# Second attention of a fused transformer block: row sums by halving additions on GpSimd instead of matmuls with ones

## The chip, the cores and the metric

The kernel runs on one core of one Trainium2 chip. The core has five engines with a queue each: TensorE (PE; its weight loads are shown as PEld), VectorE (DVE), ScalarE (ACT), GpSimd (POOL) and SyncE (SP), which only issues transfers here. Each engine takes its instructions in a fixed order and waits on semaphores for the others. The metric is device microseconds (us) of one execution; the time of a kernel is the median of its runs.

## The reference

Two layers are applied to x of 16 sequences x 128 tokens x 256 channels. The first is an attention with two key/value sources and a gated feed-forward. The second is a plain masked attention of 32 heads of 8 channels, with 8 groups of keys and values (4 heads share one), and a mixture of experts. The change lies in the second attention alone:

```
def _L1_xattn_ref(Q, K, V, attention_mask, w_q, w_k, w_v, w_o, b_o):
    ...
    scores = jnp.einsum('bnghd,bmgd->bnghm', q, k) / scale
    pad = (attention_mask == 0)[:, None, None, None, :]
    scores = jnp.where(pad, NEG_INF, scores)
    causal = jnp.tril(jnp.ones((S, S), bool))[None, :, None, None, :]
    scores = jnp.where(causal, scores, NEG_INF)
    attn = jax.nn.softmax(scores, axis=-1)
    out = jnp.einsum('bnghm,bmgd->bnghd', attn, v).reshape(B, S, D)
    return out @ w_o.T + b_o
```

The softmax needs, for each of 16 x 128 x 32 rows of 128 scores, the sum of the exponentials; the output of a head is divided by it.

## The kernel before

The kernel works through four parts: the first attention (to about 950 us), the first feed-forward (to about 1080 us), the second attention (to about 1390 us) and the experts. In the second attention a loop runs over 64 steps, n = 0 to 63, and each step handles 8 heads (two groups of 4) of one sequence: sequence b = n // 4, channel half c = n // 2 % 2. In step n the loop emits, in this order: scores(n), top(n), probs(n - 1), exp(n), values(n - 2), and between them keys for a later sequence, the projections of the next group of four sequences, the output of an earlier one, and pieces of the routing. A scheduler then places the instructions of each engine by its own estimate of their times, so the order on an engine can differ a little from the order of the program; after that the order is fixed.

What each function does, with the lines of the profile:

- keys (L973 to L987): GpSimd writes kb, the keys masked for each of the 4 heads of a group (two multiplications L975 for each sequence, two buffers); TensorE projects the values, VectorE copies them into vpad (L986), where each head has its 8 columns of 32 and the rest is zero.
- scores (L989): TensorE adds the mask with an identity matmul (L997) and multiplies queries and kb (L1004) into a PSUM tile of 128 x 1024, two buffers.
- top (L1011): VectorE takes the negated maximum of each of the 8 rows of 128.
- exp (L1020): ScalarE, eight activations of 128 x 128, writes e (three buffers). The queries are on the partitions.
- probs (L1031, L1032): TensorE transposes the eight blocks of e, VectorE copies them to eT.
- values (L1035 to L1054), only for odd n, for the 16 heads of steps n - 1 and n: the loop over t, h and q (L1043 to L1051) multiplies eT with vpad for t = 0 and with ones8 for t = 1, in four column tiles of 32. So the second half of the PSUM tile o holds the sum of exponentials of each head, repeated over its 8 rows, with the channels on the partitions. VectorE takes its reciprocal (L1053) and multiplies (L1054) into oT.
- output (L1060 and after): TensorE multiplies oT with the output weights once per sequence; VectorE adds bias and residual (L1062, L1066).
- load (L906 to L916): the mask of four sequences is loaded as integers into mi, VectorE turns it into pad (0 or -1e30, L915) and combines it with the causal mask (L916).

Besides, GpSimd normalises rows for the next group (L934) and issues the scatter of routed rows (L845).

Of the kernel before, what the change touches and what calls it, by code (L numbers as in the profile page):

```python
# [9 lines left out]
F32 = mybir.dt.float32  # L10
# [3 lines left out]
I32 = mybir.dt.int32  # L14
AF = mybir.ActivationFunctionType
ALU = mybir.AluOpType
AX = mybir.AxisListType

P = 128
# [5 lines left out]
NEG = -1e30  # L25
# [10 lines left out]
def flamingo_kernel(  # L36
# [27 lines left out]
    nc = tc.nc  # L64
# [4 lines left out]
    NH, NG, HD = 32, 8, 8  # L69

    const = ctx.enter_context(tc.tile_pool(name="const", bufs=1))
    small = ctx.enter_context(tc.tile_pool(name="small", bufs=3))
    psum0 = ExitStack()
    psum = psum0.enter_context(tc.tile_pool(name="psum", bufs=2, space=bass.MemoryType.PSUM))
# [14 lines left out]
    def ps_pv(shape):  # L89
        return ps("pv", shape, 1)  # L90
# [11 lines left out]
    def kpn(ap):  # L102
        return ap.rearrange("(k p) n -> p k n", p=P)
# [7 lines left out]
    ident = const.tile([P, P], F32, name="ident")  # L111
# [127 lines left out]
    with (  # L239
# [74 lines left out]
        class Unit:  # L314
# [15 lines left out]
            def load(self):  # L330
                b = self.b
                if self.cross:
                    cx = ap.tile([P, KD, P], F32, tag="ctx", name="ctx")
                    nc.sync.dma_start(out=cx, in_=kpn(ctxT)[:, :, b * P : (b + 1) * P])
                    xx = ap.tile([P, KD * P], F32R, tag="xx", name="xx")
                    nc.sync.dma_start(out=xx.bitcast(F32), in_=xqx[b])
                    self.kv_lhs = [cx[:, k, :] for k in range(KD)]
                    self.q_lhs = [xx[:, k * P : (k + 1) * P] for k in range(KD)]
# [148 lines left out]
            def top(self, c):  # L487
                mx = small.tile([P, 4], F32, tag="mx", name="mx")
                nc.vector.tensor_reduce(mx, self.sc[c], AX.X, ALU.max, negate=True)  # L489
                self.mx = mx  # L490

            def exp(self, c):
                pscore = self.sc.pop(c)
                sums = small.tile([P, 4], F32, tag="sums", name="sums")
                e = ap.tile([P, 4, P], F32, tag="e", name="e", bufs=3)
                for j in range(4):
                    nc.scalar.activation(  # L497
                        e[:, j, :], pscore[:, j, :], AF.Exp, bias=self.mx[:, j : j + 1],
                        accum_out=sums[:, j : j + 1],
                    )  # L500
                self.e[c] = (e, sums)
# [5 lines left out]
            def divide(self, c):  # L507
                e, sums = self.e[c]
                nc.gpsimd.tensor_tensor(  # L509
                    e, e, sums[:, :, None].to_broadcast([P, 4, P]), ALU.mult  # L510
                )
# [10 lines left out]
            def values(self, c):  # L522
                eT = self.eT.pop(c)
                pv = ps_pv([P, 4, P])
                for g in range(2):
                    gg = 2 * c + g
                    nc.tensor.matmul(  # L527
                        pv[:, 2 * g : 2 * g + 2, :], self.vt[:, gg * P : (gg + 1) * P],
                        eT[:, 2 * g : 2 * g + 2, :], start=True, stop=True,
                    )  # L530
                self.pv[c] = pv
# [136 lines left out]
    NT = G * P  # L668
# [75 lines left out]
    NQ = NH // NG  # L744
# [9 lines left out]
    for j in range(B):  # L754
# [9 lines left out]
        out=before, in_=ones, pattern=[[1, P]], compare_op=ALU.is_gt, fill=0.0,  # L764
# [20 lines left out]
    def route(b0, G):  # L785
# [73 lines left out]
    cq = f1.enter_context(tc.tile_pool(name="a1c", bufs=1, side="right", reuse_waits="tile"))  # L859
    gp = f1.enter_context(tc.tile_pool(name="a1f", bufs=2, side="right", reuse_waits="tile"))  # L860
# [17 lines left out]
        out=causal, in_=causal, pattern=[[-1, P]], compare_op=ALU.is_ge, fill=NEG,  # L878
# [5 lines left out]
    for q in range(P // 32):  # L884
# [3 lines left out]
            out=rows, in_=rows, pattern=[[-HD, NQ]], compare_op=ALU.is_ge, fill=0.0,  # L888
# [3 lines left out]
            out=rows, in_=rows, pattern=[[HD, NQ]], compare_op=ALU.is_ge, fill=0.0,  # L892
            base=HD - 1, channel_multiplier=-1,
        )

    ones8 = cq.tile([P, NQ, 32], F32, name="ones8")
    vpads = [cq.tile([P, NG, NQ, 32], F32, name=f"vpad{i}") for i in range(2)]
    nc.gpsimd.memset(ones8, 0.0)
    for i in range(NQ):
        nc.gpsimd.memset(ones8[:, i, HD * i : HD * i + HD], 1.0)  # L900
    for t in vpads:
        nc.gpsimd.memset(t, 0.0)

# [2 lines left out]
    def load(g):  # L906
        cT = gp.tile([P, KD, NT], F32, tag="cT", name="cT")
        nc.gpsimd.dma_start(out=cT, in_=kpn(ctxT)[:, :, g * NT : (g + 1) * NT])
        mi = gp.tile([P, NT], I32, tag="mi", name="mi", bufs=1)
        nc.sync.dma_start(  # L910
            out=mi, in_=mask[g * NT : (g + 1) * NT].partition_broadcast(P)
        )
        comb = gp.tile([P, G, P], BF16, tag="comb", name="comb")
        pad = gp.tile([P, NT], F32, tag="pad", name="pad", bufs=1)
        nc.vector.tensor_scalar(pad, mi, 0.0, NEG, ALU.is_equal, ALU.mult)  # L915
        nc.vector.tensor_tensor(  # L916
            comb, pad.rearrange("p (b t) -> p b t", b=G),
            causal[:, None, :].to_broadcast([P, G, P]), ALU.min,
        )
        front[g] = {"cT": cT, "comb": comb}  # L920
# [42 lines left out]
        else:  # L963
            nc.scalar.copy(f[i][:, c, :], pm)

    kbs, vps, es, eTs, oTs, scs, mxs = {}, {}, {}, {}, {}, {}, {}

    def keys(b):

# [46 lines left out]
    def exp(n):  # L1016
        s, mx = scs.pop(n), mxs.pop(n)
        e = ap.tile([P, 8, P], F32, tag="e", name="e", bufs=3)
        for i in range(8):
            nc.scalar.activation(  # L1020
                e[:, i, :], s[:, i // NQ, i % NQ, :], AF.Exp, bias=mx[:, i : i + 1]
            )
        es[n] = e

    def probs(n):
# [9 lines left out]
    def values(n):  # L1035

        if n % 2 == 0:
            return
        b, c = n // 4, n // 2 % 2
        if c == 0:  # L1040
            oTs[b] = ap.tile([P, KD, P], F32, tag="oT", name="oT")
        o = psum.tile([P, 2, P], F32, tag="pv", name="ps_pv", bufs=1)
        for t in range(2):  # L1043
            for h in range(NQ):
                for q in range(4):
                    lhs = ones8[:, h, :] if t else vps[b][:, 4 * c + q, h, :]
                    nc.tensor.matmul(
                        o[32 * q : 32 * q + 32, t, :], lhs,
                        eTs[n - 1 + q // 2][:, q % 2, h, :],
                        start=(h == 0), stop=(h == NQ - 1),  # L1050
                    )  # L1051
        r = ap.tile([P, P], F32, tag="rsum", name="rsum")
        nc.vector.reciprocal(r, o[:, 1, :])  # L1053
        nc.vector.tensor_tensor(oTs[b][:, c, :], o[:, 0, :], r, ALU.mult)  # L1054

    def output(b):
        oT = oTs.pop(b)
# [26 lines left out]
    for g in range(B // G):  # L1084
# [3 lines left out]
        for b in range(g * G, (g + 1) * G):  # L1088
# [8 lines left out]
    ap = f2.enter_context(tc.tile_pool(name="a1", bufs=2, side="right", reuse_waits="tile"))  # L1097
    psum = f2.enter_context(
        tc.tile_pool(
            name="psum1", bufs=1, space=bass.MemoryType.PSUM, reuse_waits="tile"  # L1100
        )
    )


    N1 = 4 * B
    routes = []
    for n in range(-2, N1 + 5):
        if 0 <= n < N1:
            scores(n)
            top(n)  # L1110
        if 0 <= n - 1 < N1:
            probs(n - 1)
        if 0 <= n < N1:
            exp(n)
        if 0 <= n < G:
            down(B - G + n, hd, psum.tile([P, DM], F32, tag="mm", name="ps_mm"))
            if n == G - 1:
                tp.close()
                ep = ctx.enter_context(tc.tile_pool(name="e1", bufs=2, reuse_waits="tile"))
        if 0 <= n - 2 < N1:  # L1120
            values(n - 2)
        m = n + 2
        if m % 4 == 0 and 0 <= m < N1:
            keys(m // 4)
        g, i = divmod(n + 12, 16)
        if 1 <= g < B // G:
            front_step(g, i)
        for stages in routes:
            next(stages, None)
        m = n - 4  # L1130
        if m % 4 == 3 and 0 <= m < N1:
            output(m // 4)
            for b0, count in ROUTES:
                if m // 4 == b0 + count - 1:
                    routes.append(route(b0, count))
    for stages in routes:
        for _ in stages:
# [4 lines left out]
    psum = ctx.enter_context(  # L1142
        tc.tile_pool(
            name="psum2", bufs=2, space=bass.MemoryType.PSUM, reuse_waits="tile"
        )
    )
# [4 lines left out]
    for e in range(NE):  # L1151
# [6 lines left out]
            out=xe, in_=disp[e * CAP : (e + 1) * CAP, :].rearrange("(c p) d -> p c d", p=P)  # L1158
# [5 lines left out]
        for f in range(NFC):  # L1164
            ph = ps_mm([P, CAP])
            for k in range(KD):
                nc.tensor.matmul(
                    ph, w1t[:, k, f * P : (f + 1) * P], xT[:, k, :],
                    start=(k == 0), stop=(k == KD - 1),
# [3 lines left out]
        for c in range(NCC):  # L1173
            po = ps_sc([P, DM])
            for f in range(NFC):
                nc.tensor.matmul(
                    po, hT[:, f, c * P : (c + 1) * P], w2t[:, f, :],
                    start=(f == 0), stop=(f == NFC - 1),
# [6 lines left out]
                out=out_rows,  # L1185
                out_offset=bass.IndirectOffsetOnAxis(
                    ap=xe[:, c, 2 * DM + 1 : 2 * DM + 2].bitcast(I32), axis=0
                ),
                in_=oe[:, c, :],
# [77 lines left out]
```

## Time and profile before

| what | value |
|---|---|
| median of 3 runs | 1541.4 us (1539.36 to 1542.68) |
| the profiled execution's own time | 1540.11 us |
| its span | 1538.2 us |
| mean granted TensorE clock | 0.968 |
| scores L1004, all 256 records | 1080.2 to 1379.5 us |
| L1020 exponentials (ScalarE), 512 | 139.7 us busy, 384 ns mean |
| L1011 maxima (VectorE), 64 | 78.2 us busy, 1222 ns mean |
| L1047 with ones (TensorE), 1024 records | 272 ns median of one, four at a time |
| L1053 reciprocal (VectorE), 32 | 958 ns median |
| L975 kb (GpSimd), 32 | 33.6 us busy, 1067 ns mean |

A line number names a line of the kernel. Each float32 matmul is two records in the trace, and records of TensorE overlap, so their durations don't add up; the distance from one group's start to the next one's tells more. "Idle before" names the engine that released a waiting instruction.

### The profile page before, as it was taken

The numbers are of one execution on the slowest core, as the hardware profiler recorded it, in microseconds if no ns is written. First come the engines' busy times: TensorE is split into PE (matmuls) and PEld (weight loads), VectorE is DVE, ScalarE is ACT, GpSimd is POOL, SyncE is SP. The second block draws the span as 40 slices with busy tenths as digits, with TensorE's granted clock in tenths as the row PEclk, the third lists the DMA queues.
The fourth block names the chain that finished last, engine by engine and source line by source line (L and its number), as shares of the span: only waits on it lengthen the run. The fifth ranks groups of instructions, "written<-read, shape, count | busy, mean of one in ns | idle before, by whom it ended". The sixth has DMA issues, their size and how long they took to land. (4 is left out here: it accounts for less than half of the span.)

```text
span 1538.2 us, 24640 instructions
## 1 busy us (share of the span) xinstructions
PE 1388.1 (90%) x8612; PEld 1009.7 (66%) x8612; DVE 1052.2 (68%) x2788; ACT 814.6 (53%) x2421; POOL 669.5 (44%) x574
## 2 busy tenths in 40 slices
PE   2778889798897999999999986999999999996998
PEld 1567677677675677777777764555556666664887
DVE  8888878878789777676767765433579797883100
ACT  3656566566556676666666662353355454542121
POOL 4576666666766555556565554120021312111111
PEclk9799999999999999999999998999999999996999
DMA  4300000000013100000000003400210100001662
GB/s 122 112 7 18 28 11 32 15 11 22 11 45 100 44 23 22 11 19 15 18 15 18 8 8 110 141 1 0 83 49 9 50 9 36 9 36 63 194 198 67
DMA packets 51115, 68.67 MB, mean 45 GB/s; under 512 B 5291, under 2 KB 37739, under 8 KB 50992
## 3 DMA queue, kind: packets, MB, share of 16 engines
q1 hardware_dynamic: 36912, 41.31, 9.1%
q10 hardware_dynamic: 11456, 17.63, 3.6%
q0 software_dynamic: 2624, 8.16, 1.5%
q8 instruction: 68, 1.11, 0.3%
q14 instruction: 55, 0.45, 0.1%
HBM read 50.53 MB, written 16.81 MB: 44 GB/s over the span
## 5 line engine op out<-in xcount | busy, mean ns | idle before, releaser
L509 POOL TENSOR_TENSOR e<-e,sums 128x512 f32<-128x512 f32 x128 | 139.7, 1092 | 230.8 <-DVE sums L505 120.8
L497 ACT ACTIVATE e<-ps_sc,mx 128x128 f32<-128x128 f32 x512 | 181.3, 368 | 90.1 <-DVE mx L489 82.7
L454 POOL TENSOR_TENSOR raw<-raw,q_r 128x512 f32<-128x512 f32 x192 | 207.9, 1112 | 34.1 <-DVE q_r L180 33.0
L431 DVE BATCH_NORM_STATS2 q_st<-raw 128x6 f32<-128x128 f32 x768 | 174.1, 279 | 66.9 <-ACT raw L422 66.5
L1020 ACT ACTIVATE e<-ps_sc,mx 128x128 f32<-128x128 f32 x512 | 139.7, 384 | 119.1 <-DVE mx L1011 114.1
L565 PE MATMUL ps_acc<-wp,cat 128*128 128x512 f32 x512 | 160.4, 436 | 17.6 <-POOL cat L227 15.5
L463 PE MATMUL ps_tr<-ident,raw 128*128 128x128 f32 x768 | 121.9, 288 | 46.0 <-POOL raw L454 43.8
L227 POOL TENSOR_TENSOR cat<-e_t,e_e 128x1024 fp32r<-128x1024 bf16 x64 | 136.2, 2128 | 53.7 <-DVE e_t L221 52.1
L481 PE MATMUL ps_sc<-kT,qT 128*128 128x128 f32 x1024 | 140.3, 280 | 15.0 <-ACT qT L472 15.0
L481 PEld LDWEIGHTS ps_sc<-kT,qT 128*128 128x128 f32 x1024 | 131.1, 193 | 33.0 <-ACT qT L472 27.0
L463 PEld LDWEIGHTS ps_tr<-ident,raw 128*128 128x128 f32 x768 | 96.0, 147 | 83.3 <-POOL raw L454 58.2
L519 ACT COPY eT<-ps_tr 128x512 f32<-128x512 f32 x128 | 75.4, 589 | 139.0 <-PE ps_tr L517 138.9
L975 POOL TENSOR_TENSOR kb<-kT,hmask 128x512 f32<-128x512 f32 x32 | 33.6, 1067 | 243.9 <-PE ps_sc L1004 184.6
L565 PEld LDWEIGHTS ps_acc<-wp,cat 128*128 128x128 f32 x512 | 95.9, 194 | 57.4 <-POOL cat L227 22.2
L527 PE MATMUL ps_pv<-eT,vt 128*128 128x256 f32 x512 | 132.1, 379 | 1.0 <-DVE cat_y L538 1.0
L422 ACT COPY raw<-ps_mm 128x512 f32<-128x512 f32 x192 | 113.7, 593 | 27.9 <-PE ps_mm L410 24.8
L527 PEld LDWEIGHTS ps_pv<-eT,vt 128*128 128x128 f32 x512 | 95.9, 189 | 31.2 <-issue 9.0
L538 DVE TENSOR_TENSOR cat_y<-ps_pv,r_sm 128x512 bf16<-128x512 f32 x128 | 87.1, 680 | 39.7 <-PE ps_pv L527 39.5
L472 ACT ACTIVATE qT<-ps_tr,hv 128x512 f32<-128x512 f32 x128 | 100.9, 789 | 21.8 <-PE ps_tr L463 19.8
L497 ACT ACTIVATION_READ_ACCUMULATOR e<-ps_sc,mx 128x1 f32 x512 | 105.3, 206 | 0.0
L489 DVE TENSOR_REDUCE mx<-ps_sc 128x4 f32<-128x512 f32 x128 | 87.2, 681 | 23.6 <-PE ps_sc L481 23.6
L1011 DVE TENSOR_REDUCE mx<-ps_sc 128x8 f32<-128x1024 f32 x64 | 78.2, 1222 | 25.0 <-PE ps_sc L1004 23.4
(228 smaller groups left out, 2807.3 us busy)
## 6 DMA issues: line engine op xcount, KB each, us to landing
w1t<-in_w ACTq DMA_DIRECT2D x8, 1024.0 KB, 5.0
w2t<-in_w ACTq DMA_DIRECT2D x8, 1024.0 KB, 5.6
disp<-empty SPq DMA_DIRECT2D x16, 257.0 KB, 8.5
xe<-disp SPq DMA_DIRECT2D x8, 514.0 KB, 3.6
stage<-in_wprojT SPq DMA_DIRECT2D x16, 256.0 KB, 2.7
xg<-in_x SPq DMA_DIRECT2D x4, 512.0 KB, 3.9
xb<-in_x SPq DMA_DIRECT2D x16, 128.0 KB, 2.1
ctx<-in_ctxT SPq DMA_DIRECT2D x16, 128.0 KB, 2.2
```

The source lines that it names most:

```text
L227: nc.gpsimd.tensor_tensor(dst, t[:, part], e[:, part], ALU.subtract)
L422: nc.scalar.copy(raw.rearrange("p h d -> p (h d)"), pm)
L431: nc.vector.bn_stats(self.st[:, 4 * blk + j, :], self.raws[blk][:, j, :])
L454: nc.gpsimd.tensor_tensor(src, src, self.r[:, 4 * blk : 4 * blk + 4, None].to_broadcast([P, 4, P]), ALU.mult,)
L463: nc.tensor.transpose(pt[:, j, :], src[:, j, :], ident)
L472: nc.scalar.activation(dst, pt, AF.Identity, scale=hv[:, col : col + 1], bias=hv[:, col + 1 : col + 2])
L481: nc.tensor.matmul(pscore[:, j, :], qT[:, j, :], self.kT[:, 2 * c + j // 2, :], start=True, stop=True,)
L497: nc.scalar.activation(e[:, j, :], pscore[:, j, :], AF.Exp, bias=self.mx[:, j : j + 1], accum_out=sums[:, j : j + 1],)
L509: nc.gpsimd.tensor_tensor(e, e, sums[:, :, None].to_broadcast([P, 4, P]), ALU.mult)
L527: nc.tensor.matmul(pv[:, 2 * g : 2 * g + 2, :], self.vt[:, gg * P : (gg + 1) * P], eT[:, 2 * g : 2 * g + 2, :], start=True, stop=True,)
L565: nc.tensor.matmul(self.acc, self.cat[c // 2][:, h % 8, :], wpr[self.cross, c][:, j, :, :], start=(h == 0), stop=(h == 15),)
L1020: nc.scalar.activation(e[:, i, :], s[:, i // NQ, i % NQ, :], AF.Exp, bias=mx[:, i : i + 1])
```

## The change

The sums of exponentials are no longer made by TensorE with ones8. Right after the exponentials of a step, GpSimd adds e to itself by halves, from 128 values per row to 16 (512, 256 and 128 elements per partition). For each pair of steps VectorE reduces the 16 left to one and takes the reciprocals of the 16 sums (16 elements); GpSimd repeats each reciprocal 8 times into rr; a new function divide, called one step later than values, transposes rr on TensorE into the free half of the tile o, copies it to SBUF on ScalarE, and VectorE multiplies as before. The ones8 tile and its memsets go. In load, the mask is loaded straight into pad and converted in place.

```
-    ones8 = cq.tile([P, NQ, 32], F32, name="ones8")
     vpads = [cq.tile([P, NG, NQ, 32], F32, name=f"vpad{i}") for i in range(2)]
-    nc.gpsimd.memset(ones8, 0.0)
-    for i in range(NQ):
-        nc.gpsimd.memset(ones8[:, i, HD * i : HD * i + HD], 1.0)
...
-        mi = gp.tile([P, NT], I32, tag="mi", name="mi", bufs=1)
+        pad = gp.tile([P, NT], F32, tag="pad", name="pad", bufs=1)
         nc.sync.dma_start(
-            out=mi, in_=mask[g * NT : (g + 1) * NT].partition_broadcast(P)
+            out=pad.bitcast(I32), in_=mask[g * NT : (g + 1) * NT].partition_broadcast(P)
         )
         comb = gp.tile([P, G, P], BF16, tag="comb", name="comb")
-        pad = gp.tile([P, NT], F32, tag="pad", name="pad", bufs=1)
-        nc.vector.tensor_scalar(pad, mi, 0.0, NEG, ALU.is_equal, ALU.mult)
+        nc.vector.tensor_scalar(pad, pad.bitcast(I32), 0.0, NEG, ALU.is_equal, ALU.mult)
...
     def exp(n):
...
+        if n % 2 == 0:
+            sums[n // 2] = ap.tile([P, 2, 8, 16], F32, tag="part", name="part")
+        half = ap.tile([P, 8, P // 2], F32, tag="half", name="half", bufs=1)
+        nc.gpsimd.tensor_tensor(half, e[:, :, :64], e[:, :, 64:], ALU.add)
+        nc.gpsimd.tensor_tensor(half[:, :, :32], half[:, :, :32], half[:, :, 32:], ALU.add)
+        nc.gpsimd.tensor_tensor(
+            sums[n // 2][:, n % 2], half[:, :, :16], half[:, :, 16:32], ALU.add
+        )
         es[n] = e
...
     def values(n):
...
         b, c = n // 4, n // 2 % 2
+        r = small.tile([P, 16], F32, tag="sum16", name="sum16")
+        part = sums.pop(n // 2)
+        nc.vector.tensor_reduce(r, part.rearrange("p i h t -> p (i h) t"), AX.X, ALU.add)
+        nc.vector.reciprocal(r, r)
+        rr = ap.tile([P, 16, HD], F32, tag="rr16", name="rr16", bufs=1)
+        nc.gpsimd.tensor_copy(rr, r[:, :, None].to_broadcast([P, 16, HD]))
+        o = psum.tile([P, 2, P], F32, tag="pv", name="ps_pv", bufs=1)
+        for h in range(NQ):
+            for q in range(4):
+                nc.tensor.matmul(
+                    o[32 * q : 32 * q + 32, 0, :], vps[b][:, 4 * c + q, h, :],
+                    eTs[n - 1 + q // 2][:, q % 2, h, :],
+                    start=(h == 0), stop=(h == NQ - 1),
+                )
+        pvs[n] = o, rr
+
+    def divide(n):
+
+        if n % 2 == 0:
+            return
+        b, c = n // 4, n // 2 % 2
+        o, rr = pvs.pop(n)
         if c == 0:
             oTs[b] = ap.tile([P, KD, P], F32, tag="oT", name="oT")
-        o = psum.tile([P, 2, P], F32, tag="pv", name="ps_pv", bufs=1)
-        for t in range(2):
-            for h in range(NQ):
-                for q in range(4):
-                    lhs = ones8[:, h, :] if t else vps[b][:, 4 * c + q, h, :]
-                    nc.tensor.matmul(
-                        o[32 * q : 32 * q + 32, t, :], lhs,
-                        eTs[n - 1 + q // 2][:, q % 2, h, :],
-                        start=(h == 0), stop=(h == NQ - 1),
-                    )
-        r = ap.tile([P, P], F32, tag="rsum", name="rsum")
-        nc.vector.reciprocal(r, o[:, 1, :])
-        nc.vector.tensor_tensor(oTs[b][:, c, :], o[:, 0, :], r, ALU.mult)
+        nc.tensor.transpose(o[:, 1, :], rr.rearrange("p h d -> p (h d)"), ident)
+        rT = ap.tile([P, P], F32, tag="rsum", name="rsum", bufs=1)
+        nc.scalar.copy(rT, o[:, 1, :])
+        nc.vector.tensor_tensor(oTs[b][:, c, :], o[:, 0, :], rT, ALU.mult)
...
         if 0 <= n - 2 < N1:
             values(n - 2)
+        if 0 <= n - 3 < N1:
+            divide(n - 3)
```

More of the change, by code (lines that the diff above doesn't have):

```diff
@@ L964, in qk @@
             nc.scalar.copy(f[i][:, c, :], pm)
-    kbs, vps, es, eTs, oTs, scs, mxs = {}, {}, {}, {}, {}, {}, {}
+    kbs, vps, es, eTs, oTs, scs, mxs, sums, pvs = {}, {}, {}, {}, {}, {}, {}, {}, {}
     def keys(b):
```

## The prediction

> **What bounds the kernel now.** First the page: engine totals and the 40 slices.
>
> ```profile
> PE 1388.1 (90%) x8612; PEld 1009.7 (66%) x8612; DVE 1052.2 (68%) x2788; ACT 814.6 (53%) x2421; POOL 669.5 (44%) x574
> ...
> PE   2778889798897999999999986999999999996998
> POOL 4576666666766555556565554120021312111111
> ```
>
> TensorE is busy for nine tenths of the span. The changed lines run in slices 29 to 36 (38.5 us each), where GpSimd's digits are 0 to 3. The stage window says the same; columns after the stretch are busy us and instructions:
>
> ```profile
> core 0: us, PE busy (x) PEld busy (x) DVE busy (x) ACT busy (x) POOL busy (x), PEclk, DMA share, GB/s
> 1080.00:1390.00 310.00, 305.72 (x3273) 188.98 (x3272) 244.15 (x518) 156.86 (x551) 53.18 (x50) 0.99 0.10 35
> ```
>
> In these 310 us TensorE is busy for 306 and GpSimd for 53. Matmul ends are modelled, so 306 alone does not prove a bound; the timeline decides. Columns: start, length, engine, line. This is one pair of steps (n = 32, 33) without extras:
>
> ```profile
> 1239.91 1.13 PE L1004 MATMUL ps_sc<-kb,qT 32*128 32x512 f32 x4
> ...
> 1240.97 1.09 PE L1031 MATMUL ps_tr<-ident,e 128*128 128x128 f32 x8
> ...
> 1242.43 1.13 PE L1004 MATMUL ps_sc<-kb,qT 32*128 32x512 f32 x4
> 1242.44 2.18 ACT L1020 ACTIVATE e<-ps_sc,mx 128x128 f32<-128x128 f32 x8 [2.76 <-DVE mx L1011]
> ...
> 1243.48 1.52 PE L1031 MATMUL ps_tr<-ident,e 128*128 128x128 f32 x8
> ...
> 1244.93 1.08 PE L1047 MATMUL ps_pv<-eT,vpad 128*32 128x128 f32 x32
> ...
> 1245.83 1.06 PE L1047 MATMUL ps_pv<-eT,ones 128*32 128x128 f32 x32
> 1246.81 0.11 PEld L997 LDWEIGHTS <-identb 128*128 128x128 bf16 x2 [0.20 <-issue]
> ...
> 1247.35 1.13 PE L1004 MATMUL ps_sc<-kb,qT 32*128 32x512 f32 x4
> ```
>
> From scores to scores it takes 1247.35 - 1239.91 = 7.44 us, and TensorE goes from group to group with one real stall: the transposes L1031 at 1243.48 last 1.52 us instead of 1.09, because they eat the exponentials as ScalarE makes them (1242.44 to 1244.62); the next group starts 0.31 us after the last. So the chain of a pair is: scores(even), maximum, exp(even), its transposes, values, scores of the next pair. The row sums (second L1047 line) hold TensorE from 1245.83 to 1246.8 and lie on that chain. The reciprocal L1053 and L1054 are waited for by nobody on TensorE in this pair.
>
> [...] 32 records of 0.27 us each pass in 0.9 to 1.0 us. [...] The trace, two true inputs (columns ns min/median/max):
>
> ```profile
> L227 POOL TENSOR_TENSOR xs<-e_t,e_e x16: 1642/1652/2078, 24.7 to 437.0; 128x768 fp32r<-128x768 bf16 x16
> L227 POOL TENSOR_TENSOR xx<-e_t,e_e x16: 669/675/1115, 26.7 to 438.7; 128x256 fp32r<-128x256 bf16 x16
> ```
>
> From 256 to 768 elements it grows by 977 ns: 1.91 ns per element and 186 ns fixed. [...] Four kb multiplications in a row, each with broadcast inputs, give 1.01 us each:
>
> ```profile
> 1023.06 4.03 POOL L975 TENSOR_TENSOR kb<-kT,hmask 128x512 f32<-128x512 f32 x4 [22.78 <-ACT kT L964]
> ```
>
> [...] No overlap with GpSimd adds is in this trace.
>
> **The change, part by part** (against the profiled execution: 1540.1 us, span 1538.2 plus 1.9; the median 1541.4 is 1.3 above it).
>
> *Removed from TensorE:* the ones half of L1047. Vpad half to ones half is 0.90 us, ones half to next group 0.98; I take 0.95. 32 pairs: 30.4 us, on the path. *Added to TensorE:* one transpose per pair, 1.09 / 8 = 0.13 us, 4.2 us in all. *Added to ScalarE:* a 128x128 copy from PSUM, 0.27 us (L150, 128x128). It stands before exp(even) and waits for the transpose that follows the eight of the odd step: S + 1.06 (to the first transpose) + 1.0 (eight of them) + 0.36 (from the new one's start to its reader, estimated from L149 and L150: 0.69 us for four) + 0.25 (the copy) = S + 2.65, against S + 2.53 now (1239.91 to 1242.44; S is the start of scores(even)). That 0.12 replaces the 0.13 in pairs that wait for the exponentials; it is not added twice. Net gain 30.4 - 4.2 = 26.2 us, if no new wait appears.
>
> *VectorE:* loses the 0.96 us reciprocal, gains a reduction of 256 elements (0.42, from L1011's 1.06 ns per element) and a reciprocal of 16 (0.17). Lighter by 0.37 per pair, not the bound: no gain counted. *Mask into pad without mi, ones8 memsets gone, fourth mask load behind two output rows on SP:* the memsets (0.6 us) stand before a 39 us GpSimd wait, the mask is used some 15 steps later: nothing, and at most one late combination (0.7 us).
>
> *GpSimd:* three adds per step. By the fit: 512 elements 1.16, 256 0.68, 128 0.43, plus two waits on itself of 0.05: 2.37 us per step, 152 us over 64 steps, plus 32 copies of 0.25 (memset 128x128 takes 0.20). From 53 to some 213 us of about 290: it fits on average, but order decides. Bounds for a step: 1.01 x 7/4 + 0.3 = 2.05 below (the kb rate); 3.5 above[...].
>
> **The new wait.** In the built order of the changed kernel, VectorE's reduction over a pair's partial sums is often placed straight before the maximum of the next step. VectorE is in order, so a late GpSimd holds that maximum, then the eight exponentials, then TensorE's transposes. For odd n of the form 4k+1 the reduction stands after a later maximum: no harm. For n = 4k+3 it stands before the maximum of 4k+4. In six of those (n = 15, 19, 31, 35, 47, 51) both kb multiplications of a later batch also stand between the adds of step n-1. Time from S of step n-1:
>
> - exp(n-1) ends 2.65 + 2.18 = 4.83; adds start 4.87.
> - GpSimd: 2.37 (adds) + 2.02 (kb) + 2.37 (adds of n) + 0.25 (the copy in between) = 7.01: done 11.88. exp(n) ended at about 8, so the backlog binds.
> - reduction 11.95 to 12.37, 0.30 for the one or two small operations placed after it, maximum to 13.9, exp(n+1) from 13.92.
> - Without it: S of n+1 is 5.14 (end of the transposes, 4.83 + 0.31) + 0.93 (values) + 0.97 (output L1060) + 0.53 (mask L997) = 7.57; VectorE is through L1062, L1066, L132, L133 at about 9.1; exp(n+1) from 10.3.
>
> Loss 3.6 us each, 21.7 for six, with nothing to set against it: the transposes of n+1 follow their exponentials by 0.3 us and all later TensorE work follows them. The same reckoning at n = 23 (four 1.22 us L934 operations between the adds), n = 9 (backlog of the same four earlier, partly covered by L957 projections) and n = 59 (three scatter issues of 0.97 us in the queue) gives about 2.7 each, 8. At n = 11, 27, 39, 43 projections or router work (2 to 5 us of TensorE) cover the lateness; 0 to 0.7 each, none counted. At the end TensorE waits for the last adds, reduction, copy: 2.4 + 0.4 + 0.2 + 0.3 after exp(63) against 2.2 for transposes and both halves of L1047 now: 1.1. Sum of waits 30.8.
>
> Forecast: 1540.1 - 26.2 + 30.8 = 1544.7 on the profiled execution; with 1.3 for the median, 1546. With 2.05 per step each bad pair loses 3.0, the three others 2.2, the end 1.0: 25.6, net -0.6. With 3.5 per step: 5.9 x 6 + 4.5 x 3 + 3 = 52, net +26.
>
> **Rivals.** (a) *Gain stays, waits mostly hidden; faster.* For it: GpSimd is idle 83% of the stage, and the reduction is placed where its producer was thought done. Against: the order is fixed and 7.0 us of queue do not fit into the 4 us before that maximum. The mechanism is GpSimd's speed in those places: the balance tips at about 2.05 us of adds per step; at 1.5 us half of the waits are left, 1541.4 - 26.2 + 15 = 1530; with none, 1515. Its likeliest time is 1530. (b) *GpSimd is the pace.* Adds at 3.5 us: 4 steps need 14 + 2 + 0.5 = 16.5 us against 14.2 that TensorE needs: slower everywhere, 1567. [...] Against: 213 of 290 us by the fit. (c) *A wash:* the waits eat the gain at 2.05 to 2.2 us per step: 1541. (d) *The change doesn't take the sums off TensorE:* excluded, the 512 matmuls are absent from the built order.
>
> **How the numbers follow.** Forecast (moderately slower, 1545 to 1556) 0.40; faster (a) 0.31; wash (c) 0.16; GpSimd-bound (b) 0.13. About 0.2% (3 us) is what a measurement of this kernel can tell from no change. Faster 0.31, within 0.17, slower 0.52. Range of 8 in 10: 1526 (half of the waits) to 1561; the forecast's own range is 1541 to 1557.
>
> **What would show it.** L1047 with vpad alone, about 1 us per pair. Adds of about 1.16, 0.68 and 0.43 us. The maximum waiting for GpSimd's partial sums or the reduction, 3 us or so in six places, and ScalarE's exp behind it. GpSimd about 213 us busy in the stage. Wrong if the reduction waits under 1 us in those places, or if the stage before 1080 us shifts.

## The result, and the profile after

The changed kernel takes 1576.6 us (median of 6 runs, 1571.9 to 1578.0) against 1541.4 us before: ratio 1.0227, 95% interval 1.0212 to 1.0242. It is slower, as forecast, but by 35 us where 5 were forecast. The profiled execution has a span of 1576.2 us (before 1538.2).

The page of the changed kernel, engine totals and slices:

```profile
PE 1390.5 (88%) x7620; PEld 1002.1 (64%) x7620; DVE 1050.9 (67%) x2821; ACT 819.5 (52%) x2452; POOL 835.7 (53%) x793
...
PE   2878798798988999999999978999898899885998
...
POOL 4566666667677555565656552121766766661111
PEclk9999999999999999999999988999998979885999
```

TensorE has 992 matmul records fewer and is busy for as long as before (1390.5 us, then 1388.1): its records have become longer. In the slices of the second attention (29 to 36) its granted clock reads 9, 9, 8, 9, 7, 9, 8, 8 tenths; in the kernel before it reads 9 in all of them. By the clock's records in the trace, in which only full and half occur, it stood at half for 67.9 us of the stage, and for 6.8 us in the kernel before. The window of the stage (length, then busy us and instructions of each engine, clock):

```profile
1084.00:1414.00 330.00, 293.99 (x2191) 169.34 (x2188) 235.08 (x527) 158.24 (x567) 213.34 (x266) 0.90 0.10 33
```

GpSimd is busy for 213 us, as forecast, and TensorE, busy for 306 of 310 us before, now has gaps. The waits of the stage (who waited for what: us, times, longest):

```profile
ACT e L1015 <- DVE mx L1006: 85.0, 48, 6.0
...
DVE sum L1045 <- POOL part L1023: 40.7, 15, 4.1
...
PE ps_tr L1034 <- ACT e L1015: 12.8, 9, 2.0
PE ps_pv L1067 <- POOL rr L1048: 12.2, 7, 3.5
```

VectorE's reduction L1045 waits 40.7 us for GpSimd's adds, and TensorE waits for the exponentials (L1034) and for the repeated reciprocals rr (L1067). One such place in full, the pairs n = 34 and 36 (start, length, engine, line; in brackets the idle time before and its releaser):

```profile
1274.60 1.04 POOL L970 TENSOR_TENSOR kb<-kT,hmask 128x512 f32<-128x512 f32 x1
1274.63 1.30 DVE L1082 SCALAR_TENSOR_TENSOR row<-t,tg,x 128x256 f32<-128x256 f32 x1
...
1276.32 1.26 POOL L1021 TENSOR_TENSOR half<-e 128x512 f32<-128x512 f32 x1
...
1277.77 0.72 POOL L1022 TENSOR_TENSOR half<-half 128x256 f32<-128x256 f32 x1
...
1277.86 0.33 PE L1067 MATMUL ps_pv<-ident,rr 128*128 128x128 f32 x1 [1.26 <-POOL rr L1048]
...
1278.57 0.45 POOL L1023 TENSOR_TENSOR part<-half 128x128 f32<-128x128 f32 x1
1279.06 0.42 DVE L1045 TENSOR_REDUCE sum<-part 128x16 f32<-128x256 f32 x1 [2.46 <-POOL part L1023]
...
1279.68 1.16 DVE L1006 TENSOR_REDUCE mx<-ps_sc 128x8 f32<-128x1024 f32 x1
...
1280.94 2.18 ACT L1015 ACTIVATE e<-ps_sc,mx 128x128 f32<-128x128 f32 x8 [0.76 <-DVE mx L1006]
...
1281.58 2.06 PE L1034 MATMUL ps_tr<-ident,e 128*128 128x128 f32 x8 [1.90 <-ACT e L1015]
...
1283.57 1.94 PE L1052 MATMUL ps_pv<-eT,vpad 128*32 128x128 f32 x32
...
1285.44 1.03 PE L992 MATMUL ps_sc<-comb,identb 128*128 128x512 bf16 x2
```

The chain is the one the prediction drew: adds, reduction (2.46 us late), maximum of n = 36, its exponentials, TensorE's transposes. Three things in it were not drawn. TensorE waits 1.26 us for rr (L1067), whose copy stands in GpSimd's queue behind the first add of the next step. After the second wait, values L1052 last 1.94 us (before: 1.08) and the mask L992 1.03 (0.59). And VectorE's row operation L1082, 0.45 us without adds, lasts 1.30 us beside GpSimd's kb.

The distance from the scores of n to those of n + 2 ("the pair at n"), taken from the timelines, tells where the time is. Clean pairs (n = 2, 10, 14, 18, 26, 30, 34, 42, 46, 50, 58) are 0.2 to 0.9 us shorter than before, eight of the eleven by 0.77 to 0.90. The pairs at 16, 20, 32, 36, 48, 52, the six of the prediction, are 3.4 to 5.2 us longer, those at 8, 24, 60 3.3 to 4.8. From the first scores to those of n = 62 it takes 325.97 us; before, 296.30.

The rest of the 38.0 us between the two spans is not the stage: the first scores start 4.2 us later, and the end takes 4.1 us more. The start varies over the runs below from 1080.7 to 1085.7 us with the work ahead of it unchanged (and the kernel before from 1539.3 to 1547.0 us over a set of 25 runs), so the experiments are compared by the stage, from the scores of n = 0 to those of n = 62, and by pairs. Both come from the one profiled execution, and a single pair can differ by 1.6 us between two executions without any edit near it (run 6 shows why).

### The profile page after: what moved, and what is told of

The parts are those of the page before. It is cut to its first block, busy times and chain, and to the rows that moved or that the text cites. A ratio compares the mean times of both kernels' runs of the same rounds, so it can differ in the third digit from the quotient of the medians.

```text
span 1576.2 us, 23047 instructions
## 1 busy us (share of the span) xinstructions
PE 1390.5 (88%) x7620; PEld 1002.1 (64%) x7620; DVE 1050.9 (67%) x2821; ACT 819.5 (52%) x2452; POOL 835.7 (53%) x793
## 5 line engine op out<-in xcount | busy, mean ns | idle before, releaser
L1021 POOL TENSOR_TENSOR half<-e 128x512 f32<-128x512 f32 x64 | 81.2, 1269 | 120.5 <-ACT e L1015 116.8
L1034 PEld LDWEIGHTS ps_tr<-ident,e 128*128 128x128 f32 x512 | 62.1, 150 | 61.7 <-ACT e L1015 35.0
```

## The experiments

Times are medians; each ratio is to runs of the kernel before on the same chip.

**1. The reduction moved.**

```
-        nc.vector.tensor_reduce(r, part.rearrange("p i h t -> p (i h) t"), AX.X, ALU.add)
+        red = nc.vector.tensor_reduce(r, part.rearrange("p i h t -> p (i h) t"), AX.X, ALU.add)
+        if n + 2 in tops:
+            after(red, tops[n + 2], "the maximum goes first")
```

> Changed kernel, but VectorE's reduction for odd step n is ordered behind the maximum of step n + 2; nothing else is edited. Theory 1 (a late reduction in front of the next maximum stops the exponentials and then TensorE): the six pairs starting at n = 16, 20, 32, 36, 48, 52 and the one at 24 lose their 4 to 6 us, every pair then gains about 0.76 us against the kernel before, the end still costs about 4 us: 1517 to 1530 us. Rival (GpSimd's adds or the new divide path are too slow everywhere, wherever VectorE's reduction stands): above 1555 us.

1556.2 us, ratio 1.0093 (1.0063 to 1.0123); stage 299.8 us, in the profiled execution, which is the fastest of four (1550.9, 1552.2, 1560.1, 1561.1). The order alone is worth 26 us of the stage; but more than half of what was expected is missing, and the time is just above the 1555 us of the rival. The rival's reason, slow everywhere, does not fit the pairs: ten of the eleven clean ones are 0.77 to 0.96 us shorter than before. The pair at 16 is still 3.9 us longer than before. In its trace TensorE's transpose waits 13.6 us in all for rr, which stands in GpSimd's queue behind the next add.

**2. kb moved behind the adds.**

```
+            if 4 * b - 5 in adds:
+                after(ins, adds[4 * b - 5], "the adds go first")
```

> Changed kernel, but both kb multiplications of sequence b stand on GpSimd behind the adds of step 4b - 5 instead of between them. Theory 1 with the prediction's sum: 2.0 us less GpSimd queue in front of the reduction in the six bad places, so these pairs lose about 2.3 us each instead of 4.2 to 5.9: 1560 to 1567 us. Rival (the wait is made by the speed of the adds themselves, kb does not matter): 1574 to 1579 us. Below 1550 us would say that kb is the whole cause.

1568.9 us, ratio 1.0164 (1.0147 to 1.0181). By the traces, only GpSimd's order differs from the changed kernel. The six pairs lose 1.7 to 3.0 us where they lost 3.4 to 5.2, each 1.0 to 2.2 us less: about what was expected of them. The pairs at 40 and 56 lose 3.3 and 2.3 us more instead, and the time stays 2 us above the expected range.

**3. No adds** (the sums of exponentials are left out; a constant takes their place).

```
-        nc.gpsimd.tensor_tensor(half, e[:, :, :64], e[:, :, 64:], ALU.add)
...
-            sums[n // 2] = ap.tile([P, 2, 8, 16], F32, tag="part", name="part")
+            sums[n // 2] = fixed
```

> Changed kernel without the three GpSimd adds per step; the partial sums are a constant tile, so the softmax sums are left out and the output is not divided by the real ones. Reduction, reciprocal, copy, transpose and division stay. Theory 1: only the TensorE gain is left, 26 us: 1513 to 1520 us. Rival (the divide path, that is rr, one transpose, a ScalarE copy in front of the exponentials, eats the gain by itself): above 1530 us.

1511.5 us, ratio 0.9803 (0.9783 to 0.9823); stage 265.6 us, 30.7 less than before, a little more than the 26 expected. No cost of the divide path is to be seen. So the adds, not the rest of the change, cost 325.97 - 265.56 = 60.4 us of the stage. In these are the places that VectorE's reductions get because of the adds: here, where nothing has to be waited for, the scheduler put the one of n = 35 behind the maximum of 38, not in front of that of 36.

**4. The adds alone, read by nobody**, in the kernel before.

```
+        nc.gpsimd.tensor_tensor(half, e[:, :, :64], e[:, :, 64:], ALU.add)
+        nc.gpsimd.tensor_tensor(half[:, :, :32], half[:, :, :32], half[:, :, 32:], ALU.add)
+        nc.gpsimd.tensor_tensor(
+            sums[n // 2][:, n % 2], half[:, :, :16], half[:, :, 16:32], ALU.add
+        )
         es[n] = e
```

> Kernel before with the three GpSimd adds per step put behind the exponentials, their result read by nobody; the sums still come from the matmuls with ones (and the mask is converted in place, to make room). Theory 1: GpSimd's adds harm nobody unless somebody waits for them, so 1539 to 1546 us; kb comes later but is due late. Rival (the adds slow VectorE, ScalarE or the clock [...], or hold e's buffers): 1555 us or more.

1567.6 us, ratio 1.0152 (1.0135 to 1.0169); stage 320.0 us, 23.7 more than before. The theory failed here: with adds for which nobody waits the stage is 24 us longer, although the other engines keep the order of the kernel before, but for a few operations of VectorE some 90 us ahead of the first scores. The pairs name several ways. At 20, 36 and 52 it is 1.4 to 1.5 us each, and this is VectorE: its tensor_scalar over a row, L138, takes 701 ns in the mean where the kernel before has 408. At n = 20, first in the kernel before, then here:

```profile
1184.79 1.37 DVE L138 TENSOR_SCALAR row<-row,ln_mv,ln_r 128x256 f32<-128x256 f32 x4
...
1193.62 2.52 DVE L138 TENSOR_SCALAR row<-row,ln_mv,ln_r 128x256 f32<-128x256 f32 x4
```

With L135, 0.44 instead of 0.17 us, that is 1.42 us, and the pair is 1.42 us longer; at 36 and 52 the same sum comes out within 0.02 us. At 22, 38 and 54 it is 1.6 us each; there one more stretch of 3.4 us at half clock lies in the pair than in the kernel before (see run 6). At 26, 42 and 58, 2.6 to 3.8 us, VectorE waits 3.9 to 5.3 us with the copy L840 into a row tile whose rows GpSimd still has to scatter; the scatters stand between the adds. In the pair at 16 (4.1 us) VectorE waits 1.7 us for the mask, and a stretch at half clock lies there too. The buffers of e, the last of the rivals, were not held: no exponentials start less than 6.4 us after the end of the add that reads e of three steps before, and one takes 0.38 us, as before.

**5. TensorE's wait filled**, in three of the six places, with the other three as control.

```
+        if n - 1 in (16, 32, 48):
+            for _ in range(7):
+                nc.tensor.matmul(
+                    s[:, 0], identb, f["comb"][:, j, None, :].to_broadcast([P, NQ, P]),
+                    start=True, stop=True,
+                )
```

> Changed kernel with seven more mask matmuls (about 0.27 us each, overwritten by the real ones) in front of scores n = 17, 33 and 49 only, that is inside TensorE's wait of about 2 us in the pairs starting at 16, 32 and 48; every engine's order is otherwise the same. The pairs at 20, 36 and 52 are the control. Theory (TensorE's clock falls in a wait and the 4 us of work after it pays for it): the matmuls after the wait go back to full speed (values 0.95 us instead of 1.88, mask 0.53 instead of 0.97) and these three pairs become 1.0 to 1.8 us shorter than in the changed kernel, the controls stay as they are. Rival (the slow records are something else[...]): the three pairs are as long as before or longer, by up to 0.5 us.

A single run, 1569.6 us. The pairs at 16, 32, 48 go from +5.03, +5.15, +4.26 to +3.81, +3.70, +3.08 us: 1.2 to 1.45 us shorter, though TensorE does 1.7 us more. Of the controls 20 and 52 stay within 0.02 us; 36 changes by 0.44. The pairs at 24, 28 and 38, far from the edit, change by 1.2 to 1.3 us as well, so pairs alone would not prove it. The time from the exponentials of n to the scores of n + 2 does not have that doubt: at 16, 32 and 48 it is 5.47, 5.47 and 5.20 us in the changed kernel, 4.25, 4.03 and 4.03 here, and 4.04 without adds (run 3); at 20 and 52 it is 5.47 and 5.46. TensorE at n = 32, first with the wait filled:

```profile
1257.81 1.13 PE L1005 MATMUL ps_sc<-kb,qT 32*128 32x512 f32 x4
1259.42 1.90 PE L1040 MATMUL ps_tr<-ident,e 128*128 128x128 f32 x8 [0.49 <-ACT e L1021]
1261.25 1.08 PE L1058 MATMUL ps_pv<-eT,vpad 128*32 128x128 f32 x32
1262.26 0.61 PE L998 MATMUL ps_sc<-comb,identb 128*128 128x512 bf16 x2
```

and in the changed kernel:

```profile
1258.49 1.13 PE L999 MATMUL ps_sc<-kb,qT 32*128 32x512 f32 x4
1261.61 2.05 PE L1034 MATMUL ps_tr<-ident,e 128*128 128x128 f32 x8 [1.99 <-ACT e L1015]
1263.60 1.94 PE L1052 MATMUL ps_pv<-eT,vpad 128*32 128x128 f32 x32
1265.46 1.03 PE L992 MATMUL ps_sc<-comb,identb 128*128 128x512 bf16 x2
```

The transposes start 7.76 us after the scores of n = 32 in the first and 7.77 in the second: the exponentials are as late. What is gone is the slowness after the wait. The windows of the changed kernel there (stretch, length, TensorE busy, granted clock):

```profile
1258.00:1260.00 2.00, 1.62 (x7) 1.00 0.00 0
1260.00:1262.00 2.00, 0.39 (x2) 0.62 0.00 0
1262.00:1264.00 2.00, 2.00 (x16) 0.50 0.01 4
1264.00:1266.00 2.00, 2.00 (x34) 0.50 0.00 0
1266.00:1268.00 2.00, 2.00 (x7) 0.67 0.03 8
```

With the wait filled every window from 1250 to 1268 us shows 1.00.

**6. The mask edit alone.**

> Kernel before with only the mask edit: loaded into pad and converted in place, no mi. Theory 1: costs nothing, 1539 to 1545 us, every pair as before. Rival (the load that now waits for the combination holds VectorE near n = 16, which made 4 us of the adds-alone run): the pair at 16 becomes about 4 us longer, 1544 us or more.

A single run, 1544.0 us, inside the spread of the kernel before; stage 297.4 us. The pair at 16 is 1.6 us longer, because VectorE waits there for the mask:

```profile
1165.82 0.43 DVE L914 TENSOR_SCALAR pad<-pad 128x512 f32<-128x512 int32 x1 [1.51 <-DMA pad<-in_mask]
```

So some 1.6 of the 4.1 us of that pair in run 4 come from the mask edit and not from the adds. The pair at 22 is 1.6 us shorter and the one at 54 1.6 longer, where no mask is near: behind the router's small matmuls L798 (16 of 128x8) the clock stood at half for 3.4 us, at n = 22 in the kernel before, at n = 54 in this one. Values in the pair at 22, first in the kernel before, then here:

```profile
1195.29 1.94 PE L1047 MATMUL ps_pv<-eT,vpad 128*32 128x128 f32 x32
...
1198.95 1.08 PE L1046 MATMUL ps_pv<-eT,vpad 128*32 128x128 f32 x32
```

TensorE has the same order in both. So 1.6 us at 22, 38 or 54 in one profile are no proof of an edit's effect.

**7. Late reduction, and rr copied by VectorE.**

```
-        nc.gpsimd.tensor_copy(rr, r[:, :, None].to_broadcast([P, 16, HD]))
+        nc.vector.tensor_copy(rr, r[:, :, None].to_broadcast([P, 16, HD]))
```

> The kernel of the first experiment (reduction behind the maximum of n + 2) with the copy rr on VectorE instead of GpSimd. Theory: 16 us of that run were TensorE's transpose waiting for rr at the end of GpSimd's queue; these waits go, 1535 to 1545 us. Rival (what is left there is contention and late transfers, not rr): 1552 us or more.

1546.1 us, ratio 1.0022 (1.0014 to 1.0029), 1 us above the expected range; stage 294.8 us. TensorE's wait for rr falls to 3.0 us. Still 29 us of the adds' cost are there, although hardly anyone waits for their result any more. The clock stood at half for 29.8 us of the stage (2.0 in run 3). One place, at n = 20:

```profile
1173.95 1.03 POOL L977 TENSOR_TENSOR kb<-kT,hmask 128x512 f32<-128x512 f32 x1
1173.97 1.30 DVE L1093 SCALAR_TENSOR_TENSOR row<-t,tg,x 128x256 f32<-128x256 f32 x1
...
1176.25 0.69 DVE L142 TENSOR_SCALAR ln_v<-ln_mv 128x4 f32<-128x4 f32 x1
...
1176.93 1.21 DVE L1015 TENSOR_REDUCE mx<-ps_sc 128x8 f32<-128x1024 f32 x1
```

and the same row operation in run 3, with GpSimd quiet:

```profile
1168.50 0.45 DVE L1078 SCALAR_TENSOR_TENSOR row<-t,tg,x 128x256 f32<-128x256 f32 x1
```

The row operation is 0.85 us longer and ends 0.29 us after GpSimd's kb; L142 lasts 0.69 instead of 0.17 us. Both stand in front of the maximum. In the window 1084 to 1380 us the mean of the row operation is 881 ns here, 757 in the changed kernel, 497 in run 3; that of the maximum (a reduction) is 1206 to 1222 in all of them.

**8. The same with kb behind the adds.**

> As the run before it, and kb behind the adds of step 4b - 5. Theory: with all three waits on GpSimd's queue gone, what is left over the 1511 us without adds is the stretching of VectorE's small operations (about 10 us) and late scatters: 1525 to 1540 us, faster than the kernel before. Rival (GpSimd's throughput): not under 1543 us.

1546.4 us, ratio 1.0012 (1.0003 to 1.0022): the expectation failed, and the time is where the rival put it; kb's place is worth nothing in sum. Only GpSimd's order differs from run 7. At 20, 36, 48 and 52 the row operation is back at 0.45 us, and these pairs are 0.05 to 1.7 us shorter; the one at 40 is 3.7 us shorter. But the one at 16 is 1.4 us longer and the one at 56 6.0: at 56 VectorE's small L844 and L846 take 1.05 and 1.09 us beside the moved kb (0.16 and 0.23 without adds), and the clock falls behind them. The stretching went elsewhere.

**9. Late reduction, rr on VectorE, and the row operation behind the maximum.**

```
+        if 4 * b + 8 in tops:
+            after(ins, tops[4 * b + 8], "the maximum goes first")
...
-        m = n - 4
+        m = n - 5
```

> The kernel with the late reduction and rr on VectorE, and besides the output of a sequence is issued one step later with its row operation (scalar_tensor_tensor, two SBUF inputs) ordered behind the maximum of step 4b + 8. Theory (what is left there is VectorE operations that stand in front of a maximum and are stretched from 0.45 to 1.3 us by a GpSimd instruction running beside them, plus the clock fall after the wait): the pairs starting at 16, 20, 32, 36, 48, 52 lose 0.7 to 2.5 us less, the stage gets about 8 to 12 us shorter, 1534 to 1540 us. Rival (these pairs are held by something else): 1544 us or more.

1539.5 us (20 runs, 1537.3 to 1542.6), ratio 0.9976 (0.9968 to 0.9983): 0.24% faster than the kernel before, the best version found. The stage is 284.7 us, 10.1 less than in run 7, as expected. The six pairs are now 0.3 to 1.5 us shorter than before; those at 22, 38 and 54, where the moved operations gather, are 2.3 to 4.7 us longer, and from the scores of n = 62 to the end it takes 169.5 us instead of 161.8, which gives most of the stage's gain back. The edit moves the whole output, not the row operation alone, and every engine's order differs from run 7; what the stretching was worth in it is not shown (see run 12).

**10. Only half of the pairs** take their sums from GpSimd (n = 4k + 1), the others from the matmuls with ones, as before.

```
+        if n // 2 % 2 == 0:
             half = ap.tile([P, 8, P // 2], F32, tag="half", name="half", bufs=1)
...
+        if c:
...
+                        lhs = ones8[:, h, :] if t else vps[b][:, 4 * c + q, h, :]
...
+            return
```

> Changed kernel in which only the pairs n = 4k + 1 take their sums from GpSimd; the pairs n = 4k + 3, whose reduction stood in front of the maximum of 4k + 4, go back to the matmuls with ones. Theory: half of the gain stays (16 pairs of about 0.8 to 0.95 us, 13 to 15), the waits for the reduction go, some stretched VectorE operations remain in the pairs at 20, 36, 52 (about 1 us each) : 1529 to 1536 us, faster than both kernels. Rival (GpSimd's adds cost by their number wherever they stand): half of the loss, 1555 to 1560 us.

1564.2 us, ratio 1.0150 (1.0136 to 1.0164), above both the expected range and the rival's. Half of the adds were gone, but the reduction stood badly again: the scheduler had now put it before the maximum of 4k + 2. It waits 2.1 us in the pair at 30 and 5.0 us in the one at 42, and these pairs are 2.6 and 5.2 us longer.

**11 and 12. The same, with the edits of runs 1 and 7; then also with those of run 9.**

> The kernel with sums from GpSimd for the pairs n = 4k + 1 alone, and now its reduction ordered behind the maximum of n + 2 and the copy rr on VectorE. In the run before it the pairs starting at 14, 26, 30, 42 and 46 were 2.6 to 5.2 us longer, with the reduction in front of the maximum of 4k + 2. Theory (the wait had only moved to another maximum): these five come down to 0 or below, the sum over all pairs falls by 25 to 35 us: 1528 to 1538 us, faster than before and at least as fast as the late version with all sums on GpSimd (1546). Rival (the adds cost by their number): 1550 us or more.

> As the run before it, with the output of a sequence one step later and its row operation behind the maximum of step 4b + 8. Theory: another 3 to 8 us from the pairs at 16, 20, 32, 36, 48, 52, where VectorE operations beside an add or a kb multiplication still stand in front of a maximum: 1524 to 1534 us. Rival (with half of the adds gone there is little left to stretch): within 3 us of the run before it.

1548.0 us, ratio 1.0033 (1.0017 to 1.0049), and 1541.6 us, ratio 0.9987 (0.9979 to 0.9995): both above the expected range, neither at its rival. In run 11 the pairs at 14, 30 and 46 come down to -0.9 us, as expected; those at 26 and 42 stay at +5.0 and +4.9. There it is the scatters:

```profile
1206.02 1.11 POOL L852 DMA_INDIRECT disp<-row,slot_s  x1 [2.04 <-DVE slot_s L850]
1207.16 1.28 POOL L1035 TENSOR_TENSOR half<-e 128x512 f32<-128x512 f32 x1
...
1208.62 1.01 POOL L852 DMA_INDIRECT disp<-row,slot_s  x1 [0.18 <-issue]
...
1210.56 0.99 POOL L852 DMA_INDIRECT disp<-row,slot_s  x1 [0.17 <-issue]
...
1212.20 0.98 POOL L852 DMA_INDIRECT disp<-row,slot_s  x1 [0.17 <-issue]
...
1215.88 0.17 DVE L847 COPY row<-number 128x4 int32<-128x4 int32 x1 [5.11 <-issue]
```

Four scatters of a tile alternate with the adds of one step, from 1206.0 to 1212.2 us, and VectorE's copy into the row tile, in front of the maximum of n = 27, has to wait; the same copy in the pair at 42 is released after 5.0 us by the transfer of the last scatter. In the kernel before the same four take from 1208.8 to 1212.8 us with nothing between them, and the copy waits 1.6 us. Putting the scatters ahead of the adds was not tried.

In run 12 the pairs at 26 and 42 come down to -1.8 us, but those at 22, 38 and 54 go up to 3.7 to 3.9. And the pairs at 20, 36 and 52 are 2.2 to 2.3 us shorter than in run 11, nearly as much as from run 7 to run 9 (2.4 to 2.5), although the row operation takes 0.48 us in both. That points to the moved work, more than to the stretching of that operation, in the step from run 7 to run 9.

## Why the prediction was right in direction and wrong in size

**Right.** The direction, by a margin of 5 us between a gain of 26 and losses of 31. The gain on TensorE: 26.2 us foreseen; without adds the stage is 30.7 us shorter. The list of places: all six pairs named are bad, and nearly alike. The point in time without adds: exp(36) 10.3 us after the scores of n = 34, measured 10.26 (run 3). GpSimd's busy time, 213 us, in part by luck: the 152 us for the adds held 6 us of waits, and the adds themselves take 159 us, of which 5 lie outside the window. That GpSimd is not the pace: it is idle 114 us waiting for exponentials. Rivals (b) and (d) fall with that; (a) spoke of 15 us of waits or fewer, (c) of a wash. Two small sums in the prediction are off, and nothing hangs on them: 1.06 + 1.0 + 0.36 + 0.25 is 2.67, not 2.65, and 1.01 x 7/4 + 0.3 is 2.07, not 2.05.

**Wrong: the step "Loss 3.6 us each, 21.7 for six, with nothing to set against it".** The mechanism holds, the term was too small. By the trace, for n = 34 to 38, times from the scores of n = 34:

| | forecast | no adds (run 3) | changed kernel |
|---|---|---|---|
| exp(36) without / with adds | 10.3 / 13.9 | 10.26 | 14.51 |
| from exp(36) to the scores of n = 38 | the same in both | 4.04 | 5.47 |

So this place costs 4.25 us of lateness and 1.43 us after it, 5.7 where 3.6 were counted; over the six the lateness is 3.8 to 4.5 us and what comes after it 1.2 to 1.4 us. The excess in lateness has three parts. The adds are slower: 1.16 + 0.68 + 0.43 was fitted; the medians are 1.27, 0.73 and 0.45 us,

```profile
L1021 POOL TENSOR_TENSOR half<-e x64: 1253/1267/1310, 1089.2 to 1418.4; 128x512 f32<-128x512 f32 x64
L1022 POOL TENSOR_TENSOR half<-half x64: 715/726/1169, 1090.5 to 1419.7; 128x256 f32<-128x256 f32 x64
L1023 POOL TENSOR_TENSOR part<-half x64: 447/454/648, 1091.4 to 1420.6; 128x128 f32<-128x128 f32 x64
```

and one step of GpSimd takes 2.69 us from add to add, not 2.37: 0.08 us lie between one add and the next, where 0.05 was estimated. The upper bound of 3.5 us for a step, on which rival (b) stood, was the author's assumption, drawn from no trace. (Columns: minimum, median, maximum in ns, then first and last start.) This makes the queue in each place 0.3 us longer than the 7.01 us of the sum. At 16 and 32 it is 0.5 us longer still, because VectorE's L911 and L1082 started first there and the add L1022 and a kb beside them took 1.17 and 1.32 us, not 0.73 and 1.04. At 20 and 36 the adds start 0.4 us later, because TensorE was still slow from the place before (the scores of n = 34 took 1.55 us, not 1.13). The second excess, 1.2 to 1.4 us, is TensorE's clock: the prediction let "all later TensorE work follow" at the speed it had, and the clock falls to half after the wait: at n = 32 it reads 0.50 from 1262 to 1266 us. Run 5 shows that this is the cause: with the wait filled it reads 1.00 there, and the 1.43 us at n = 32 are gone.

**What was left out.** The cost of the adds, pair by pair (changed kernel less run 3): the six places with the pairs behind 16 and 32 33.5 us (21.7 forecast), 8, 24 and 60 15.0 us (8 forecast, for the same three delays), all other pairs 11.9 us (none forecast). Of the 30.7 us between 60.4 and the 29.7 forecast for the stage, 11.8 us lie in the six (3.5 us more lateness, 8.3 us with the slow clock behind it), 7.0 us in the three, and 11.9 us in the other pairs. In 22, 38 and 54 (1.7 to 1.8 us each) VectorE's operations are stretched beside the adds, and 4.0 to 4.8 us at half clock lie there too; which of them it is was not separated. On VectorE the prediction wrote "Lighter by 0.37 per pair, not the bound: no gain counted". Nor was a loss counted there: that VectorE's operations keep their length beside the adds was the author's estimate. For three groups it holds: in the window 1084 to 1380 us the maxima take 1206 ns in the mean (1222 in the kernel before), the copies to eT 678 (683), the multiplications into oT 280 (288). It does not hold for the row operation (L1082, 757 ns instead of 480), nor for L180 (0.70 to 0.81 us instead of 0.16) and L816 (once in three 1.05 us instead of 0.18). What sets these apart from the first was not shown. Run 4 shows what it costs where such operations stand on the way to TensorE: 1.4 to 1.5 us in each of the pairs at 20, 36 and 52.

The end was 1.1 us in the sum; it is 4.1 us longer in the changed kernel and 1.8 in run 3. What part is a wait and what differs from run to run was not separated; neither were the shares of stretched operations, scatters and slow clock in the 29 us that run 7 left.

## What to carry to other kernels

Taking work off the bound engine pays only if the engine that gets it never stands in front of that engine's chain: look in the built order for every instruction that waits for the new work, at what is queued behind it, and order it behind the chain's own instructions. A wait on TensorE is to be priced with the slow clock that can follow, here 1.2 to 1.4 us behind each of the six waits of about 2 us. And an engine that was idle is not free: GpSimd's adds, with nobody waiting for them, made operations of VectorE (L138, 701 ns in the mean instead of 408) and GpSimd's own scatters late (VectorE waited 3.9 to 5.3 us for them), and most of the 24 us of run 4 come from that and from the slow clock behind it.

## What the runs showed of the hardware that was not expected

- In the traces of the two kernels every record of the clock but the last lasts a whole multiple of 3.413 us, and in the stage it stood at half for one to three cells at a time (a cell is one such 3.413 us). Take the cells of the two stages at full clock: of those in which TensorE's records cover under 45% of the time, all 4 were followed by half clock; of those with 45 to 80%, 6 of 13; above that 2 of 143, and each of these 2 holds the router's small matmuls (L798, 128x8), during which the trace counts TensorE as busy.
- So the length of a wait does not decide alone. At n = 32 waits of 1.80 and 1.99 us, with 1.8 us of work between them, left a cell covered to 53%, and the clock fell; in run 5 a wait of 1.79 us, with the filling behind it, was followed by full clock in every window to 1268 us; in run 7 at n = 20 TensorE was busy for 2.66 of the 4 us from 1176 on, and the clock fell (0.76 from 1180 to 1182 us, 0.50 from 1182 to 1184).
- At n = 36 the clock stood at half from 1281 to 1291 us, although TensorE was busy without a gap from 1282 us on (2.00 us in each window of 2); at n = 32 it was full again from 1267 us.
- In the changed kernel the row operation L1082 took 1.30 to 1.31 us in four places where a kb of GpSimd, 1.04 to 1.05 us long, had started up to 0.03 us before it, and 0.48 us where no GpSimd instruction ran beside it. L816 (128x32) took 1.05 us at 1379.3 us, where an add L1021 still had 1.01 us to run, and 0.18 in the other two steps. The length added, 0.83 and 0.87 us, is nearly the same for both, as is what was left of the GpSimd instruction (1.0 us), while their own lengths differ by more than twice. Where VectorE had started first (L911 at n = 16 and 32), GpSimd's add was the longer one, 1.17 us instead of 0.73.
